# Context attentions of a two-layer perceiver: partial sums of the third head group joined on VectorE, weights of the last group summed in four parts

## The chip, the cores and the metric

The kernel runs on one core of a Trainium2 chip. A core has TensorE (PE in the profile; PEld is its weight load), VectorE (DVE), ScalarE (ACT), GpSimd (POOL), SyncE (SP, which here only issues DMAs) and 16 DMA engines. Matmuls write PSUM; all other data is in SBUF or in the chip's memory. The metric is the device time of one execution in microseconds (us), as the median of several runs.

## The reference

A batch of one, 512 query rows of 512 channels (`x`), a context of 8192 rows of 512 channels, and two layers. Each layer adds three things to `x`: a cross attention from `x` to the context, a self attention, and a mixture of 8 expert MLPs. The change touches only the two cross attentions, which have 16 heads of 32 channels each. The first is, cut to what matters (the second has no norm of q and k, and its mask comes from another input):

```python
q = _ln(q, qn_w, qn_b) * scale
k = _ln(k, kn_w, kn_b)
attn = jnp.einsum('bihd,bjhd->bhij', q, k)
attn = jnp.where(padding_mask[:, None, None, :], attn, -jnp.inf)
p = jax.nn.softmax(attn, axis=-1)
ctx = jnp.einsum('bhij,bjhd->bihd', p, v).reshape(b, s1, c)
out = ctx @ Wo.T + bo
```

The softmax needs, for each head and query, the sum of the exponentials over all keys (the denominator) and the sum of the exponentials times the values. The kernel forms both without dividing first, and divides at the end.

## The kernel before

Both attentions go through one function, `attend_slots`. It picks the tiles of 128 keys of the context that hold anything, at most 15 of them (`n = SLOTS = 15`), and works on the 16 heads in four groups of four (`NG = 4`, `GH = 4`). Its main loop runs over `at = 0 .. 59`, with `g, i = divmod(at, n)`: group `g`, key tile `i`. In the text (g, i) names a step of this loop; (3, 2) is the third key tile of the last group. One step does this:

- `score` (L939): four matmuls, one for each head, put 128 keys x 512 queries into four PSUM tiles `sc`. `subtract` (L800) takes off the largest score of each query. The four heads use different rows of the PE array and run side by side; a line "sc L939 x8" in the profile is four weight loads and four matmuls.
- `exp` (L1089): ScalarE turns each `sc` into a quarter of the SBUF tile `pT` (128 x 2048 numbers). `pT` has 5 buffers.
- For the group after, TensorE also makes scores the other way round (`scm`, L957), of which VectorE takes the maxima. These run ahead of their group, so the end of group 2 and all of group 3 have none.
- `accumulate` (L1044): four matmuls, side by side in different columns of the array, multiply `pT` with the values. For groups 0 to 2 each step has its own PSUM tile, which VectorE adds to the SBUF tile `o` (L1052). Group 3 sums in one PSUM tile `k.sums`. Where no `scm` are left, a step does this for the `pT` of two steps before (`accumulate(2)`).
- `add_up` (L1063): adds the `pT` of up to four steps into one tile `four` (5 buffers), on GpSimd for groups 0 to 2 and on VectorE for group 3. What is left is the list `parts[g]`. For groups 0 to 2 it has five members: steps 0-3, 4-7, 8-11, 12-13, and 14 alone. For group 3 it has six: 0-3, 4-7, 8-11, and 12, 13 and 14 alone.
- `denominators` (L1072): for each member of `parts[g]` four matmuls with a matrix of ones, side by side in the columns of the array, sum over the keys into one PSUM tile `den`.

Work of a group that is finished is put into `fillers` with the step at which it is due; each step takes at most one. For groups 0 to 2 these are `denominators` (L1127, due 3 steps after the group's last step; ScalarE then takes the logarithm of `den`, L1078), `divide` (4 steps after: an exponential on ScalarE, L1083, then a product and an added bias on GpSimd, L1084 and L1086), and `outputs` (L889, the product with the output weights, which VectorE adds to `x`, L895; for group 2 due 13 and 14 steps after). So group 2's denominators come in step (3, 2) and its outputs in steps (3, 12) and (3, 13).

The last group's denominators are written out by hand: two parts after step (3, 13), two after (3, 14), then `accumulate` for step 13, the last two parts, and `accumulate` for step 14. Then `finish_part` (L859 calls `divided`, L848) does two halves of 256 queries one after the other: logarithm and exponential of the denominator on ScalarE (`inverse`, L202 and L203), the product on VectorE (L850), the bias on ScalarE (L853). The four `outputs` of the last group and the norm of `x` follow.

A planner orders the instructions. Each engine gets a list; from the order of the program, the planner takes the first instruction that is ready by its own estimate of times, so one that would have to wait is passed by others. Each engine then works through its list. `tc.issue_after(ins)` puts everything traced inside it behind `ins` on the same engine; `pin` keeps the program's order.

PSUM tiles come from two sets, 4 of tag "s" and 3 of tag "m". `tile_s` takes them in a cycle of seven, so a step's four `sc` tiles can be written about one step ahead of the exponentials.

## Time and profile before

| what | us |
|---|---|
| runs shown: median (lowest, highest) of 3 | 1437.43 (1436.31, 1438.10) |
| the profiled execution: its time | 1435.61 |
| the profiled execution: span, first to last instruction | 1433.70 |
| PE `den` L1072, 216 matmuls in both attentions, mean of one | 0.592 |
| DVE `four` L1063 (128x2048 added), x18, each | 2.29 |
| POOL `four` L1063 (128x2048 added), x60, each | 4.55 |
| POOL L1084 and L1086 in `divide`, each | 1.29 and 1.57 |
| DVE L1052 (128x512 added), each | 0.68 |

The span is what the trace shows; the time has 1.91 us more that lie around it. The first attention's last group runs from about 344 to 394 us of the span, the second's from about 1103 to 1153 us.

How to read it: the chain of waits is the work that ended last, followed back from the end; a line has its start, its length, the engine, the tile and the line of the program. The timeline has every instruction, with the idle time of its engine before it and what ended it in square brackets. In both, neighbours of one kind are merged, and "x" counts them.

### The profile page before, as it was taken

What the parts mean: (1) busy time and instruction counts of PE and PEld (TensorE: products, weight loads), DVE (VectorE), ACT (ScalarE), POOL (GpSimd) and SP (SyncE); (2) the same over time, 40 slices, a digit from 0 to 9 for tenths busy, and PEclk for the clock granted to TensorE, in tenths of its full rate; (3) what the DMA queues carried; (4) which work ended last, traced back from release to release, by engine and by line L of the source; (5) the groups of instructions that cost most, each with busy time, mean ns of one, the idle gap of its engine ahead of it and who ended that gap; (6) DMA issues with size and microseconds to landing.
All of it is one profiled execution on the core that took longest, in us unless ns stands there. A gap on an engine that the chain in (4) does not pass through costs nothing.

```text
span 1433.7 us, 24957 instructions
## 1 busy us (share of the span) xinstructions
PE 1401.6 (98%) x9797; PEld 860.4 (60%) x9797; DVE 695.5 (49%) x1983; ACT 583.1 (41%) x1168; POOL 425.2 (30%) x359
## 2 busy tenths in 40 slices
PE   7989999999999999999999999999999999999997
PEld 3434444443244558999999766644444235499993
DVE  5558598985523424111111226769886525741112
ACT  2657466667732353111111131157667732321221
POOL 2150078987010110200001110058988010020002
PEclk9999999999999999999999999999999999989999
DMA  8455200000050005987889451000000050068575
GB/s 249 153 190 150 74 31 1 1 2 1 2 212 1 16 16 186 389 307 263 273 280 298 160 174 30 30 1 1 2 1 2 1 191 1 2 237 328 197 248 184
DMA packets 94267, 175.15 MB, mean 122 GB/s; under 512 B 5496, under 2 KB 32182, under 8 KB 92348
## 3 DMA queue, kind: packets, MB, share of 16 engines
q1 hardware_dynamic: 87004, 151.43, 31.5%
q0 software_dynamic: 6416, 19.94, 3.9%
q10 hardware_dynamic: 720, 2.10, 0.4%
q8 instruction: 79, 1.29, 0.4%
q14 instruction: 48, 0.39, 0.1%
HBM read 162.72 MB, written 9.68 MB: 120 GB/s over the span
## 4 chain that ended last, share of the span: by engine, by line
PE 88%; DVE 2%; ACT 1%; DMA 1%; issue 1%; POOL 0%; POOLq 0%; ACTq 0%
PE hps L2364 12%; PE y L2385 12%; PE sc L939 11%; PE acc L1044 8%; PE prj L1612 4%; PE pk L1421 4%; PE ops L889 4%; PE scm L957 4%; PE sc L957 3%; PE pv L1233 3%; PE den L1072 3%; PE pva L1548 2%; PE sc L800 2%; PE pk L1233 1%; PE y L2342 1%; PE pv L1457 1%
## 5 line engine op out<-in xcount | busy, mean ns | idle before, releaser
L1089 ACT ACTIVATE pT<-sc,kbias 128x512 f32<-128x512 f32 x480 | 288.3, 708 | 96.2 <-PE sc L800 85.7
L968 DVE CUSTOM_DVE_ANT_0 masked<-scm,krowb 128x512 f32<-128x512 f32 (+2 forms) x400 | 213.9, 591 | 40.0 <-PE scm L957 38.1
L939 PE MATMUL sc<-qTf,kTf 32*128 32x512 f32 x960 | 216.8, 621 | 1.5 <-DVE tops L968 1.5
L2364 PE MATMUL hps<-tokens,w 128*128 128x160 f32 (+11 forms) x1408 | 193.3, 293 | 0.0
L957 PE MATMUL scm<-kTf,qTf 32*128 32x512 f32 (+2 forms) x800 | 189.3, 539 | 0.0
L2364 PEld LDWEIGHTS hps<-tokens,w 128*128 128x128 f32 x1408 | 184.1, 191 | 2.7 <-issue 1.0
L2385 PE MATMUL y<-hT,w 128*128 128x160 f32 (+11 forms) x1280 | 176.2, 296 | 0.0
L2385 PEld LDWEIGHTS y<-hT,w 128*128 128x128 f32 x1280 | 169.7, 192 | 2.5 <-issue 0.8
L1063 POOL TENSOR_TENSOR four<-four,pT 128x2048 f32<-128x2048 f32 x36 | 163.9, 4553 | 1.6
L939 PEld LDWEIGHTS sc<-qTf,kTf 32*128 32x128 f32 x960 | 73.6, 183 | 95.7 <-DVE tops L968 42.5
L1044 PE MATMUL acc<-pT,vNf 128*32 128x512 f32 x960 | 127.8, 604 | 0.0
L968 DVE CUSTOM_DVE_ANT_0 masked<-sc,krowb 128x512 f32<-128x512 f32 (+2 forms) x176 | 98.6, 614 | 55.8 <-PE sc L957 55.2
L1063 POOL TENSOR_TENSOR four<-pT 128x2048 f32<-128x2048 f32 x24 | 109.3, 4554 | 54.1 <-ACT pT L1089 54.1
L2623 DVE TENSOR_TENSOR hT<-sg,hps 128x264 f32<-128x264 f32 (+7 forms) x64 | 28.0, 437 | 191.7 <-ACT sg L2622 177.1
L2622 ACT ACTIVATE sg<-hps 128x264 f32<-128x264 f32 (+7 forms) x64 | 25.3, 396 | 174.5 <-PE hps L2364 169.7
L957 PEld LDWEIGHTS scm<-kTf,qTf 32*128 32x128 f32 x800 | 86.1, 184 | 15.5 <-issue 6.3
L800 PE MATMUL sc<-shift,ones 3*128 3x512 bf16 (+3 forms) x544 | 93.2, 367 | 0.0
L2416 POOL DMA_DIRECT2D answers_d<-yb x17 | 9.6, 564 | 240.8 <-ACT yb L2403 240.8
L1052 DVE TENSOR_TENSOR o<-o,acc 128x512 f32<-128x512 f32 x84 | 57.3, 682 | 20.4 <-PE acc L1044 20.4
L1044 PEld LDWEIGHTS acc<-pT,vNf 128*32 128x32 f32 x960 | 19.3, 108 | 70.3 <-DVE tops L968 34.7
L1233 PE MATMUL pv<-wkvf,cslot 128*128 128x512 f32 x120 | 55.6, 613 | 3.0 <-issue 1.9
L1421 PE MATMUL pk<-cslot,wkf 128*128 128x256 f32 (+1 forms) x256 | 55.5, 370 | 0.0
(390 smaller groups left out, 1828.8 us busy)
## 6 DMA issues: line engine op xcount, KB each, us to landing
w<-in_L_ffn_W SPq DMA_DIRECT2D x94, 1024.0 KB, 6.6
mi<-in_mask SPq DMA_DIRECT2D x32, 512.0 KB, 4.2
cslot<-in_ctxT SPq DMA_DIRECT2D x40, 256.0 KB, 3.3
answers_d<-yb POOLq DMA_DIRECT2D x13, 256.0 KB, 4.6
answers_d<-zero POOLq DMA_DIRECT2D x9, 256.0 KB, 3.0
wkvf<-in_L_xattn_WkvT SPq DMA_DIRECT2D x8, 256.0 KB, 6.6
wof<-in_L_xattn_WoT SPq DMA_DIRECT2D x2, 1024.0 KB
wide<-in_L_attn_wk SPq DMA_DIRECT2D x4, 512.0 KB, 5.6
```

The source lines that it names most:

```text
L800: nc.tensor.matmul(ps, lhsT=ones16[r, :], rhs=k.shifts[g][r, 0:w], start=start, stop=stop)
L889: nc.tensor.matmul(ps, lhsT=k.o[g][:, t * P : (t + 1) * P], rhs=wo()[:, g, :], start=not direct, stop=True)
L939: nc.tensor.matmul(ps, lhsT=kT[HD * h : HD * (h + 1), g, i * P : (i + 1) * P], rhs=qT[HD * h : HD * (h + 1), g, :], start=True, stop=stop,)
L957: nc.tensor.matmul(ps[:, at : at + w], lhsT=qT[HD * h : HD * (h + 1), g, t * P : (t + 1) * P], rhs=kT[HD * h : HD * (h + 1), g, lo : lo + ...
L968: nc.vector.tensor_tensor_reduce(masked[:, 0:w], ps[:, at : at + w], krow[:, lo : lo + w], 1.0, -BIG, ALU.add, ALU.max, accum_out=tops[g % ...
L1044: nc.tensor.matmul(acc[HD * h : HD * (h + 1), :], lhsT=vN[:, i, g * P + HD * h : g * P + HD * (h + 1)], rhs=pT[:, h, :], start=alone or i ...
L1063: engine.tensor_tensor(to, parts[g][-1], pT, ALU.add)
L1089: nc.scalar.activation(pT[:, h, :], ps, AF.Exp, bias=kbias[:, i : i + 1])
L1233: last = nc.tensor.matmul(ps.rearrange("p (g n) -> p g n", g=NG), lhsT=src[:, c, s % 2, :], rhs=wkv[:, :, c, i * P : (i + 1) * P], start=( ...
L1421: end = nc.tensor.matmul(ps[:, j], lhsT=wk[:, g, c], rhs=src[:, c], start=(c == 0), stop=(c == NC - 1))
L2364: end = nc.tensor.matmul(ps[:, j, 0:k], lhsT=w1[:, c, f * P : (f + 1) * P], rhs=tokens[:, c, starts[r] : starts[r] + k], start=(c == 0), s ...
L2385: nc.tensor.matmul(accs[0][:, d, 0:k], lhsT=w2[:, f, d * P : (d + 1) * P], rhs=hT[:, f, 0:k], start=(c == 0 and f == 0 and d % 2 == 0), st ...
```

## The change

It touches the second half of `attend_slots` and two small functions above it.

- Group 2, joining: in step (3, 1), behind the addition of the group's last values (`k.added`, the last L1052), VectorE adds part 14 to part 12-13 (`join(2, 3, 4)`), then does step (3, 1)'s own `add_up`, then adds part 0-3 to part 4-7 (`join(2, 1, 0)`). `issue_after` fixes this order on VectorE. `parts[2]` is left with three members instead of five: 0-7, 8-11, 12-14.
- Group 2, due times: its denominators are due 4 steps after the group's last step instead of 3, and `divide` 5 instead of 4. Groups 0 and 1 keep theirs.
- Group 2, dividing: the product and the bias in `divide` go to VectorE instead of GpSimd.
- Group 3, joining: after the additions of steps 7 and 11 VectorE joins two parts each time, so that `parts[3]` ends with four members, 0-11, 12, 13 and 14, instead of six.
- Group 3, the end: no denominators after steps (3, 13) and (3, 14). After the loop come `accumulate` for step 13, the denominators of 12, 13 and 14, `accumulate` for step 14, and the denominators of 0-11.
- Group 3, dividing: both halves' `inverse` come first, then both halves' product and bias.

```diff
         def add_up(g, i, pT):
 
-            engine = nc.gpsimd if g < NG - 1 else nc.vector
-            if i % 4 == 0 or i >= (n - 1 if g < NG - 1 else (n - 1) // 4 * 4):
+            final = g == NG - 1
+            if i % 4 == 0 or i >= n - (3 if final else 1):
                 parts[g].append(pT)
                 return
...
-            engine.tensor_tensor(to, parts[g][-1], pT, ALU.add)
+            added = (nc.vector if final else nc.gpsimd).tensor_tensor(to, parts[g][-1], pT, ALU.add)
             parts[g][-1] = to
+            if final and i in (n // 2, n - 4):
+                join(g, 1, 0)
+            return added
+
+        def join(g, to, of):
+
+            ins = nc.vector.tensor_tensor(parts[g][to], parts[g][to], parts[g][of], ALU.add)
+            parts[g].pop(of)
+            return ins
...
         def divide(g):
 
             nc.scalar.activation(dens[g], dens[g], AF.Exp, scale=-1.0)
+            if g == NG - 2:
+                nc.vector.tensor_tensor(k.o[g], k.o[g], dens[g], ALU.mult)
+                nc.vector.tensor_scalar(k.o[g], k.o[g], bv[:, g : g + 1], None, ALU.add)
+                return
...
-            add_up(g, i, pT)
+            if g == NG - 1 and i == 1:
+                with tc.issue_after(k.added.ins):
+                    joined = join(NG - 2, 3, 4)
+                    with tc.issue_after(joined.ins):
+                        late_add = add_up(g, i, pT)
+                        with tc.issue_after(late_add.ins):
+                            join(NG - 2, 1, 0)
+            else:
+                add_up(g, i, pT)
             if i == n - 1 and g < NG - 1:
+                rest = 4 if g == NG - 2 else 3
                 fillers.extend((
-                    (at + 3, lambda g=g: denominators(g, range(len(parts[g])), len(parts[g]))),
-                    (at + 4, lambda g=g: divide(g)),
+                    (at + rest, lambda g=g: denominators(g, range(len(parts[g])))),
+                    (at + rest + 1, lambda g=g: divide(g)),
...
-            if g == NG - 1 and i >= n - 2:
-
-                lone = n - (n - 1) // 4 * 4
-                whole = (n - 1) // 4
-                end = whole + lone
-                denominators(g, range(0, whole - 1) if i == n - 2 else range(whole - 1, end - 2), end)
         accumulate(1)
-        denominators(NG - 1, range(end - 2, end), end)
+        denominators(NG - 1, (1, 2, 3), True, False)
         accumulate(1)
+        denominators(NG - 1, (0,), False, True)
         for _, f in fillers:
             f()
+        r = slice(0, S // 2), slice(S // 2, S)
+        d = late().tile([P, S], F32, name="d", tag="d", bufs=1)
+        k.o[NG - 1] = late().tile([P, S], F32, name="o", tag="o", bufs=2)
         for i in range(2):
-            r = slice(i * S // 2, (i + 1) * S // 2)
-            k.finish_part(NG - 1, r, k.sums[NG - 1][:, r], dens[NG - 1][:, r])
+            inverse(d[:, r[i]], dens[NG - 1][:, r[i]])
+        for i in range(2):
+            k.divided(NG - 1, r[i], d[:, r[i]], k.sums[NG - 1][:, r[i]])
         k.outputs(NG - 1, range(NT))
```

More of the change, by code (lines that the diff above doesn't have):

```diff
@@ L846, in begin, with divided @@
             k.sums[g] = [pacc.tile([P, S], F32, name=name, tag=name) for name in ("acc", "den")]
-        def divided(g, r, d, acc, den):
-            inverse(d[:, r], den)
-            nc.vector.tensor_tensor(k.o[g][:, r], acc, d[:, r], ALU.mult)
+        def divided(g, r, d, acc):
+            nc.vector.tensor_tensor(k.o[g][:, r], acc, d, ALU.mult)
             if bv is not None:
@@ L858, in finish_part @@
                 k.o[g] = late().tile([P, S], F32, name="o", tag="o", bufs=2)
-            divided(g, r, late().tile([P, S], F32, name="d", tag="d", bufs=1), acc, den)
+            d = late().tile([P, S], F32, name="d", tag="d", bufs=1)
+            inverse(d[:, r], den)
+            divided(g, r, d[:, r], acc)
         def finish(g, pieces=1):
@@ L895, in outputs @@
                     nc.vector.tensor_tensor(x[:, t, :], x[:, t, :], ps, ALU.add)
-        k.tile_s, k.subtract, k.shift_of = tile_s, subtract, shift_of
+        k.tile_s, k.subtract, k.shift_of, k.divided = tile_s, subtract, shift_of, divided
         k.begin, k.finish, k.finish_part, k.outputs, k.quotient = begin, finish, finish_part, outputs, quotient
@@ L1051, in accumulate @@
             elif alone:
-                nc.vector.tensor_tensor(k.o[g], k.o[g], acc, ALU.add)
+                k.added = nc.vector.tensor_tensor(k.o[g], k.o[g], acc, ALU.add)
         def add_up(g, i, pT):
-            engine = nc.gpsimd if g < NG - 1 else nc.vector
-            if i % 4 == 0 or i >= (n - 1 if g < NG - 1 else (n - 1) // 4 * 4):
+            final = g == NG - 1
+            if i % 4 == 0 or i >= n - (3 if final else 1):
                 parts[g].append(pT)
@@ L1062, in add_up, with denominators @@
                 to = late().tile([P, GH, S], F32, name="four", tag="four", bufs=5)
-            engine.tensor_tensor(to, parts[g][-1], pT, ALU.add)
+            added = (nc.vector if final else nc.gpsimd).tensor_tensor(to, parts[g][-1], pT, ALU.add)
             parts[g][-1] = to
-        def denominators(g, which, end):
+            if final and i in (n // 2, n - 4):
[5 more added lines that the diff above has]
+            return ins
+        def denominators(g, which, first=True, last=True):
+            if first:
+                dens[g] = tile_s(name="den")
             for j in which:
-                if j == 0:
-                    dens[g] = tile_s(name="den")
                 for h in range(GH):
@@ L1073, in denominators @@
                         dens[g][HD * h : HD * (h + 1), :], lhsT=k.ones32, rhs=parts[g][j][:, h, :],
-                        start=(j == 0), stop=(j == end - 1),
+                        start=first and j == which[0], stop=last and j == which[-1],
                     )
@@ L1135, in attend_slots @@
                 fillers.pop(0)[1]()
-            if g == NG - 1 and i >= n - 2:
-                lone = n - (n - 1) // 4 * 4
-                whole = (n - 1) // 4
-                end = whole + lone
-                denominators(g, range(0, whole - 1) if i == n - 2 else range(whole - 1, end - 2), end)
         accumulate(1)
-        denominators(NG - 1, range(end - 2, end), end)
+        denominators(NG - 1, (1, 2, 3), True, False)
         accumulate(1)
+        denominators(NG - 1, (0,), False, True)
         for _, f in fillers:
             f()
+        r = slice(0, S // 2), slice(S // 2, S)
+        d = late().tile([P, S], F32, name="d", tag="d", bufs=1)
+        k.o[NG - 1] = late().tile([P, S], F32, name="o", tag="o", bufs=2)
         for i in range(2):
-            r = slice(i * S // 2, (i + 1) * S // 2)
-            k.finish_part(NG - 1, r, k.sums[NG - 1][:, r], dens[NG - 1][:, r])
+            inverse(d[:, r[i]], dens[NG - 1][:, r[i]])
+        for i in range(2):
+            k.divided(NG - 1, r[i], d[:, r[i]], k.sums[NG - 1][:, r[i]])
         k.outputs(NG - 1, range(NT))
```

## The prediction

> **What bounds the kernel now.** I read the page's busy times and chain first, then the chain of waits and the timeline in the last head group of both context attentions, and last the busy times of one stretch. The page:

> ```profile
> PE 1401.6 (98%) x9797; PEld 860.4 (60%) x9797; DVE 695.5 (49%) x1983; ACT 583.1 (41%) x1168; POOL 425.2 (30%) x359
> PE 88%; DVE 2%; ACT 1%; DMA 1%; issue 1%; POOL 0%; POOLq 0%; ACTq 0%
> ```

> TensorE is the bound almost everywhere, so matmuls taken away can count, if nothing else holds the stage. The chain of waits in the second attention's last group (start, us, work):

> ```profile
> 1109.84 4.29 PE den L1072 x40
> ...
> 1143.12 1.85 PE den L1072 x16
> 1144.97 1.07 PE sc L939 x8
> 1146.05 0.22 PE sc L800 x4
> 1146.26 0.99 PE acc L1044 x8
> 1147.26 1.72 PE den L1072 x16
> 1148.98 0.86 PE acc L1044 x8
> 1149.83 1.84 PE den L1072 x16
> ...
> 1151.76 0.39 ACT d L202
> ...
> 1153.08 0.52 ACT o L853
> ```

> Group 2's five parts take 4.29 us in one piece, 0.858 a part; the last group's six take 1.85 + 1.72 + 1.84 in three pieces. A plain step is 1.07 + 0.22 + 0.99 = 2.28 us. The first attention has the same lengths (4.29 at 351.39; 1.85, 1.72 and 1.84 at the end). The timeline says what the other engines do meanwhile:

> ```profile
> 1102.80 4.55 POOL L1063 TENSOR_TENSOR four<-pT 128x2048 f32<-128x2048 f32 x1
> 1107.63 0.69 DVE L1052 TENSOR_TENSOR o<-o,acc 128x512 f32<-128x512 f32 x1 [1.59 <-PE acc L1044]
> 1109.18 2.29 DVE L1063 TENSOR_TENSOR four<-pT 128x2048 f32<-128x2048 f32 x1 [0.87 <-ACT pT L1089]
> 1111.57 2.29 DVE L1063 TENSOR_TENSOR four<-four,pT 128x2048 f32<-128x2048 f32 x1
> 1114.20 0.60 ACT L1078 ACTIVATE d<-den 128x512 f32<-128x512 f32 x1 [2.80 <-PE den L1072]
> 1114.83 0.63 ACT L1083 ACTIVATE d<-d 128x512 f32<-128x512 f32 x1
> 1115.44 23.23 ACT L1089 ACTIVATE pT<-sc,kbias 128x512 f32<-128x512 f32 x40
> ```

> While TensorE does the 4.29 us, ScalarE runs dry for 2.80. After it, 40 exponentials run without a gap: (23.23 - 0.71) / 39 = 0.577 us apart, 2.31 a step, hardly slower than TensorE's 2.28. ScalarE is a second bound, close behind. The stretch from the last addition of group 2's values to the last addition of its outputs (us, then busy PE, PEld, DVE, ACT, POOL with counts, granted clock, DMA share, GB/s):

> ```profile
> 1107.63:1142.65 35.02, 35.02 (x288) 9.56 (x288) 22.86 (x13) 30.62 (x53) 2.84 (x2) 1.00 0.01 2
> ```

> VectorE has 12.2 us free there, and the change fills them.

> **Part by part.**

> *Group 2's denominators.* Two parts fewer: 2 x 0.858 = 1.72 us of TensorE per attention. It is worth that much only if ScalarE can use it. From (3, 2)'s exponentials at about 1109.1 (a run of 26 ends at 1111.41, its last four took 2.3) it has eleven steps to do up to (3, 12) and 1.24 us of logarithm and exponential: 11 x 2.31 + 1.24 = 26.7, so it could end at 1135.8 where it ended at 1138.67. That is 2.9 us of room, more than 1.72. Taken: 1.72; bounds 0 (ScalarE holds the pace) and 1.72.

> [...]

> *Group 2's joins.* They run on VectorE behind the L1052 that ends at 1108.32. Their inputs are there: GpSimd's last part ends at 1107.35, the exponentials of (2, 14) are older. One 128x2048 addition behind another takes 2.35 (a pair is shown at 1124.98 with 4.69). First join, the addition of (3, 1), second join: 1108.32 + 3 x 2.35 = 1115.4. Queued behind them are the additions of (3, 2) and (3, 3), which end at about 1117.7 and 1120.1 instead of 1113.9 and 1120.2; they free `pT` buffers that are written five steps later, after 1122, so nobody waits.

> But the denominators due in (3, 3) need the second join first, and TensorE comes to them at 1109.84 + 2.28 = 1112.1, before the join ends. The planner passes over what isn't ready: in the trace ScalarE's logarithm and exponential of `divide` stand ahead of exponentials that come before them in the program (1114.20 against 1115.44). So I expect the scores of (3, 4) and (3, 5) ahead of `den`, the 2.57 us of `den` at about 1115.7, and no idle TensorE. If the planner's times err, TensorE stands up to the difference; cost taken 0, bounds 0 to 3.3 an attention.

> *Divide on VectorE.* GpSimd's 1.28 + 1.57 go; the product is like L1052 (0.69), the bias between the 0.55 and 0.81 of the 128x512 L259: 1.2 to 1.5 on VectorE. Hidden: `o` is ready at about 1121, the outputs come after 1135. Uncovered, it would cost its own 1.5.

> *Last group's joins.* Two additions of 2.29. VectorE in the stretch: 22.86 + 4 x 2.29 + 1.3 = 33.3, while the stretch shrinks to 35.02 - 1.72 = 33.3. It is exactly full. In order: the additions of 5, 6, 7 and the join end at 1130.6, those of 9, 10, 11 and the join at about 1140.0, the four outputs' additions (0.65 each) at 1142.7. What is late next is the PSUM of those outputs, which the scores of (3, 14) need at 1141.4 to 1141.8: of seven tiles four hold outputs and three are free, so one output must be added before, and it is, at 1140.7. Cost 0 with 0.9 us to spare. The part 0-11 is needed last of all, at about 1148.

> *The end.* Before, from 1143.12 to ScalarE's start at 1151.76: six parts 1.85 + 1.72 + 1.84, a step 2.28, an accumulate 0.86, 0.09 of hand-over: 8.64. After: a step 2.28, accumulate 13 0.86, parts 12, 13, 14 2.57, accumulate 14 0.86, part 0-11 with its hand-over 0.98, 0.08: 7.63. Gain 1.01, less than two parts, because accumulate 14 used to run under ScalarE's logarithm and now stands ahead of it. Part 14 needs the last exponential, 1.29 + 2.42 = 3.7 us in; its turn comes at 4.9.

> *Both inverses first.* Before, the first half's bias starts 1.32 after ScalarE's first logarithm. Now the second logarithm and exponential come between: starts 0, 0.41, 0.73, 1.13 (a 0.51 instruction is followed 0.41 after its start, so neighbours overlap 0.1), bias at about 1.45. Loss 0.13, bounds 0.04 (full overlap) and 0.32 (none). The second half is ready no later, and VectorE's chain behind the first half sets the pace. The end gains 1.01 - 0.13 = 0.88; bounds 0.69 and 0.97.

> *DMAs.* None is added. SP's next weights waited for accumulate 14 (issued 394.06 and 1152.51). The last reader of the old tiles becomes part 0-11, which ends earlier than accumulate 14 did, so they move up with the chain or more.

> Sum: 2 x (1.72 + 0.88) = 5.2 us. The profiled execution took 1435.61 (span 1433.70, 1.91 around it): 1430.4. The runs' median is 1.82 above it, so 1437.43 - 5.2 = 1432.2.

> **Rivals.**

> *TensorE waits for the join (slower).* If the planner leaves `den` at its place, TensorE stands from 1112.1 to 1115.4, 3.3 us for 1.72 saved. With the end's 0.88 that is +0.7 an attention: 1438.8. From 2.6 us of standing on, an end of the join after 1114.7, the change loses; each microsecond more on VectorE costs 2. For it: the join ends later than that by the rows above; against it, the passing over just shown.

> [...]

> *ScalarE holds the pace.* The middle gains nothing, the end 0.88: 1437.43 - 1.8 = 1435.7. For it, 2.31 against 2.28; against it, the 2.80 idle.

> *VectorE is late.* If its list slips 2 us, the scores of (3, 14) wait 1.1: 2 x (2.60 - 1.1) = 3.0, 1434.4. For it, the sum of 33.3 in 33.3; against it, that few of its results are awaited.

> **How the numbers follow.** Forecast 0.56, at 1432.2, its own range 1430.5 to 1434. VectorE late 0.12, ScalarE 0.12, TensorE waiting 0.20, of which 0.12 beyond +0.2%, since its additions come behind a full VectorE. About 0.2% (2.9 us) is what a measurement can tell from no change. Faster: 0.56 and half of 0.12, 0.62; same: 0.06 + 0.12 + 0.08 = 0.26; slower 0.12. The range 1429.8 to 1437.8 takes in the first three cases with the runs' own spread of 1.8 and leaves most of the fourth out.

> **What would show it.** Right: `den` of group 2 as one piece of 2.57 us; ScalarE's idle time before L1078 near 1.1 instead of 2.80 (it has 4.29 - 2.80 = 1.49 in hand when `den` begins, and 2.57 - 1.49 = 1.1); `den` behind scores of (3, 4) or (3, 5); four parts at the end, ScalarE's first L202 at about 7.6 us after the last outputs. Wrong: an idle TensorE released by VectorE's `four` before L1072 or before the scores of (3, 14), or ScalarE without a gap from (3, 2) on.

## The result, and the profile after

| | before | after |
|---|---|---|
| median of the first runs, us | 1437.11 (4 runs, 1436.31 to 1438.10) | 1444.78 (4 runs, 1442.09 to 1446.60) |
| ratio | | 1.0044 [1.0029, 1.0060] |
| profiled execution: time, span, us | 1435.61, 1433.7 | 1444.87, 1443.1 |
| its mean granted clock | 0.993 | 0.988 |

The change makes the kernel slower by 7.7 us. Timed again on two chips it was slower by 7.7 and 5.6 us: 1.0051 [1.0032, 1.0071] and 1.0048 [1.0030, 1.0066]. Below, the third group is group 2 of the code and the last group is group 3.

The page of after, busy times and shares of the chain that ended last by engine:

```profile
PE 1403.6 (97%) x9733; PEld 861.4 (60%) x9733; DVE 718.6 (50%) x1995; ACT 582.7 (40%) x1168; POOL 419.0 (29%) x355
PE 84%; DVE 3%; DMA 2%; issue 2%; ACT 1%; POOL 1%; POOLq 0%; SPq 0%; DVEq 0%; ACTq 0%
```

TensorE executes 64 matmul records fewer and is busy 2.0 us longer, so what is left took more time a piece. Each of these matmuls stands in the trace as two records (ten that are put in below appear as x20). So "sc x8" in the chain is four matmuls in eight records, and not four weight loads and four matmuls, as the section on the kernel before has it. `den` has 336 records before, 168 matmuls in both attentions, and not 216. The counts below are records: the 40 and 24 of the third group's `den` are 20 and 12 matmuls. The chain of waits of after, second attention, from the third group's last values on (start, us, work):

```profile
1113.70 0.54 issue
1114.24 2.29 DVE four L1072
1116.53 2.20 DVE four L1064
1118.73 2.21 DVE four L1072
1120.94 0.04 issue
1120.98 4.32 PE den L1082 x24
1125.31 1.07 PE sc L940 x8
```

The chain leaves TensorE and runs over VectorE: join, late addition, join, then `den`. `den` now has 24 records instead of 40, and yet takes 4.32 us where 40 took 4.29. The timeline of after has the same matmuls in both attentions, the first with the scores and values ahead of them (start, us, instruction, count, idle time before and what ended it):

```profile
352.45 1.22 PE L940 MATMUL sc<-qTf,kTf 32*128 32x512 f32 x7
353.41 0.39 PE L800 MATMUL sc<-shift,ones 3*128 3x512 bf16 x3
353.51 0.59 PE L940 MATMUL sc<-qTf,kTf 32*128 32x512 f32 x1
353.94 0.38 PE L800 MATMUL sc<-shift,ones 3*128 3x512 bf16 x1
354.24 1.06 PE L1045 MATMUL acc<-pT,vNf 128*32 128x512 f32 x8
357.65 2.78 PE L1082 MATMUL den<-four,ones 128*32 128x512 f32 x24 [2.34 <-DVE four L1072]
...
1120.98 4.32 PE L1082 MATMUL den<-four,ones 128*32 128x512 f32 x24 [2.35 <-DVE four L1072]
```

Both times TensorE stands idle for 2.34 us until the join ends; such an idle stretch is called a stand from here on. In the first attention the 24 then take 2.78, in the second 4.32. There the granted clock is 0.50 from 1120.73 us on for 3.41 us, a half-clock stretch; in the first attention it stays 1.00. ScalarE in the second attention of after:

```profile
1125.38 0.60 ACT L1088 ACTIVATE d<-den 128x512 f32<-128x512 f32 x1 [5.43 <-PE den L1082]
1126.01 0.63 ACT L1093 ACTIVATE d<-d 128x512 f32<-128x512 f32 x1
1126.62 20.91 ACT L1103 ACTIVATE pT<-sc,kbias 128x512 f32<-128x512 f32 x36
```

It runs dry for 5.43 us, where it was 2.80 before. The chain of waits at the end of the first attention, after:

```profile
387.11 1.07 PE sc L940 x8
388.18 0.22 PE sc L800 x4
388.40 1.85 PE acc L1045 x16
390.25 2.58 PE den L1082 x24
392.82 0.86 PE acc L1045 x8
393.68 0.86 PE den L1082 x8
```

The last group's four parts stand in the order that was forecast, with no wait between them.

I laid TensorE's accumulations and outputs of after against those of before, one by one, in the first attention. Ahead of the third group's `den` after is 1.13 us late (a half-clock stretch at 212.79 us, in code that is the same), behind it 2.47, at the last group's outputs 1.44. The stretch around the third group's `den` is called the middle, the one from there to the outputs the end: the middle costs 1.34 and the end gains 1.03. The 1.34 is the stand of 2.34, plus 0.5 in which the scores of (3, 3) wait for a PSUM tile, minus the 4.29 - 2.78 = 1.51 saved. The wait of 0.5 shows in the lines above: the fourth head's scores start alone at 353.51, when an exponential of ScalarE ends (353.50), and this step takes 2.78 us (from 351.46 to 354.24, values to values) where a plain one takes 2.28. In the second attention the middle costs 2.88, half clock included. At full clock the change would cost 2 x (1.34 - 1.03) = 0.6 us; some 5 to 7 us more are to be found.

### The profile page after: what moved, and what is told of

Its sections match the earlier page's. It is cut to its first block, busy times and chain, and to the rows that moved or that the text cites. A ratio compares the mean times of both kernels' runs of the same rounds, so it can differ in the third digit from the quotient of the medians.

```text
span 1443.1 us, 24827 instructions
## 1 busy us (share of the span) xinstructions
PE 1403.6 (97%) x9733; PEld 861.4 (60%) x9733; DVE 718.6 (50%) x1995; ACT 582.7 (40%) x1168; POOL 419.0 (29%) x355
## 3 DMA queue, kind: packets, MB, share of 16 engines
q8 instruction: 78, 1.28, 0.4%
## 4 chain that ended last, share of the span: by engine, by line
PE 84%; DVE 3%; DMA 2%; issue 2%; ACT 1%; POOL 1%; POOLq 0%; SPq 0%; DVEq 0%; ACTq 0%
PE hps L2386 11%; PE y L2407 11%; PE sc L940 10%; PE acc L1045 8%; PE prj L1634 4%; PE pk L1443 4%; PE scm L958 4%; PE ops L890 4%; PE sc L958 3%; PE pva L1570 2%; PE pv L1255 2%; PE den L1082 2%; PE sc L800 2%; PE y L2364 1%; PE vps L1821 1%
## 5 line engine op out<-in xcount | busy, mean ns | idle before, releaser
L800 PE MATMUL sc<-shift,ones 3*128 3x512 bf16 (+3 forms) x544 | 94.3, 368 | 0.0
L1255 PE MATMUL pk<-wkvf,cslot 128*128 128x512 f32 x120 | 56.3, 613 | 0.0
```

Source lines behind the costliest of these rows:

```text
L800: nc.tensor.matmul(ps, lhsT=ones16[r, :], rhs=k.shifts[g][r, 0:w], start=start, stop=stop)
L1255: last = nc.tensor.matmul(ps.rearrange("p (g n) -> p g n", g=NG), lhsT=src[:, c, s % 2, :], rhs=wkv[:, :, c, i * P : (i + 1) * P], start=( ...
```

## The experiments

Every kernel was timed beside the kernel before on the same chip. Times are medians, ratios with their 95% intervals.

**The kernel before, unaltered.**

> The kernel before, unchanged, as a control: its granted clock beside its time in several runs. In its profile the clock is at half in 4 stretches (one of them after the last matmul), in the changed kernel's in 10, and one more half-clock window of 3.4 us costs up to 1.7 us. Theory 'the wait' (the loss is TensorE standing 2.34 us in each attention for the join, and what follows from it): time 1437 +- 1 and clock 0.993 each time. Theory 'the windows' (most of the loss is half-clock windows that fall differently from run to run, whatever the code): the clock varies between 0.988 and 0.993 and the time between 1436 and 1444 with it, some 1.4 us for 0.001.

Measured: 1436.57 us, 0.9996 [0.9987, 1.0006]. A measurement of this size can tell some 1.5 us from nothing.

**The change with the denominators two tiles later.**

```diff
-                rest = 4 if g == NG - 2 else 3
+                rest = 6 if g == NG - 2 else 3
```

> The changed kernel with group 2's denominators due 6 steps after the group's last step instead of 4, and divide 7, so that the second join is done before TensorE comes to them. 'The wait': no idle TensorE ahead of group 2's den, 2 x 2.34 us of standing and 2 x 0.6 of held-up scores go, and the half-clock den of the second attention with them: 1437 or less, faster than the kernel before if the end's 2 x 1.0 gain is real. 'The windows': still 1440 to 1445 with a clock of 0.988 to 0.990. 'ScalarE holds the pace': no idle TensorE, but the middle gains nothing, about 1435 to 1438.

Measured: 1437.56, 0.9995 [0.9986, 1.0005]. The stand is gone, and with it the loss. Timeline of this kernel, first attention:

```profile
356.05 1.22 PE L940 MATMUL sc<-qTf,kTf 32*128 32x512 f32 x7
...
357.10 0.59 PE L940 MATMUL sc<-qTf,kTf 32*128 32x512 f32 x1
...
362.41 1.07 PE L1045 MATMUL acc<-pT,vNf 128*32 128x512 f32 x8
363.29 2.76 PE L1082 MATMUL den<-four,ones 128*32 128x512 f32 x24
```

`den` has no idle time before it. The middle gains 1.21 in both attentions, not the whole 1.72: the wait of 0.5 in the scores of (3, 3) is still there.

**The end alone**: the last group's four parts, its joins and both inverses first; the third group as before.

```diff
-            if g == NG - 2:
-                nc.vector.tensor_tensor(k.o[g], k.o[g], dens[g], ALU.mult)
-                nc.vector.tensor_scalar(k.o[g], k.o[g], bv[:, g : g + 1], None, ALU.add)
-                return
...
-            if g == NG - 1 and i == 1:
...
-            else:
-                add_up(g, i, pT)
+            add_up(g, i, pT)
...
-                rest = 4 if g == NG - 2 else 3
+                rest = 3
```

> The kernel before with the last group's end alone (four parts, two joins, both inverses first); group 2 as before. Predicted for this part: -0.88 an attention, read from the two traces: -1.03. 'The wait': 1437.1 - 2.1 = 1435.0. 'The windows': anything from 1434 to 1441, by its clock. A third theory, 'the end' (the new end costs time in what follows, by a longer idle TensorE before the norm): slower than 1438.

Measured: 1436.62, 0.9995 [0.9984, 1.0005]. Its trace gains 0.92 us at each of the two ends, 1.8 together, which is hardly more than the times can tell.

**The middle alone**: the third group's joins and divide as in the change, the last group as before.

```diff
-            if final and i in (n // 2, n - 4):
-                join(g, 1, 0)
...
+            if g == NG - 1 and i >= n - 2:
+                denominators(NG - 1, (0, 1) if i == n - 2 else (2, 3), i == n - 2, False)
...
-        denominators(NG - 1, (1, 2, 3), True, False)
+        denominators(NG - 1, (4, 5), False, True)
         accumulate(1)
-        denominators(NG - 1, (0,), False, True)
...
```

> The changed kernel with the last group's end as before (six parts, no joins in group 3, halves one after the other); group 2's joins, its due times and its divide as changed. 'The wait': the middle's +1.34 in each attention, and a den at half clock after 2.3 us of standing in one or both: 1437.1 + 2.7 to 1437.1 + 6.1, 1440 to 1443. 'The windows': the same middle, but the rest of the difference goes with the clock. 'The end': 1439.8 or less.

Measured: 1441.34, 1.0029 [1.0019, 1.0039]. The middle alone brings a loss of 4.2 us and the end alone none. Its trace has half clock straight behind both stands: `den` takes 4.23 and 4.08 us there, near the 4.32 above, and the middle costs 2.79 and 2.64 instead of 1.34. But the two halves of the change add up to 4.2 - 0.5 = 3.7 us, by the medians, where both together cost 5.6 to 7.7; what the rest is these two runs don't show.

**The change once more**, beside the next three.

> The changed kernel again, unaltered, on the chip and in the rounds of the three that follow. 'The wait' (TensorE stands 2.34 us ahead of the third group's denominators in each attention, and the granted clock halves behind it): 1444.8 again, 1442 to 1447, 1.003 to 1.006 of the kernel before. 'The windows' (the half-clock stretches fall where they like, and the four first runs of the change had more of them than is usual): 1437 to 1441.

Measured: 1446.02, 1.0051 [1.0032, 1.0071].

**The stand filled**: ten matmuls of the identity, which nobody reads, ahead of the denominators.

```diff
                 dens[g] = tile_s(name="den")
+                if g == NG - 2:
+                    for _ in range(10):
+                        tc.keep_in_program_order(nc.tensor.matmul(dens[g][:, 0:P], lhsT=ident, rhs=ident, start=True, stop=True))
```

> The changed kernel with ten 128x128 products of the identity (10 x 0.21 = 2.1 us of work that nobody reads) put on TensorE ahead of the third group's denominators, into the tile that these then overwrite: the join still ends when it did, the denominators still wait 0.2 us for it, but TensorE is busy through most of the 2.34 us. If the halved clock behind the stand is caused by the standing, and is worth 1.2 to 1.6 us an attention: 2.4 to 3.2 us less than the changed kernel, some 1441.5 against 1444.5, and a granted clock of 1.00 at the denominators. If the loss is the stand alone and the half clock is chance: the same as the changed kernel, within 0.7. Where the ten fillers end later than the join: up to 0.3 us an attention more.

Measured: 1439.08, 1.0007 [0.9995, 1.0019], 6.9 us below the change on the same chip. The join ends no earlier; TensorE only works meanwhile. Timeline of this kernel, second attention:

```profile
1113.91 2.50 PE L1082 MATMUL den<-ident 128*128 128x128 f32 x20
1116.34 2.78 PE L1085 MATMUL den<-four,ones 128*32 128x512 f32 x24
```

The idle time is gone and the 24 matmuls take 2.78. Against before the middle costs 1.35 in each attention and the end gains 1.03, so that + 0.6 is due; +0.7 was measured. The wait itself cost little here; what the filling takes away is the idleness. The filling was expected to bring 2.4 to 3.2 and brought more than twice that here, so it was timed again further down.

**One join moved early**, to the third group's thirteenth tile.

```diff
-                    joined = join(NG - 2, 3, 4)
+                    joined = join(NG - 2, 2, 3)
...
-                        with tc.issue_after(late_add.ins):
-                            join(NG - 2, 1, 0)
...
+            if g == NG - 2 and i == 12:
+                join(NG - 2, 1, 0)
```

> The changed kernel with the join of the third group's first two parts moved from the last of VectorE's three late operations to the third group's thirteenth tile, where VectorE has 1.8 to 2.7 us idle between two additions to o; the join of the last two parts stays at the last group's second tile and ends at 353.1 in the first attention, and TensorE reaches the denominators at 355.3. 'The wait': no stand of TensorE any more, den as one piece of 2.57 us without idle time; the time goes to that of the kernel with the denominators two tiles later (1437.6) or below, by the sum of the prediction to 1432. 'VectorE': the join at the thirteenth tile holds the next addition to o by up to 0.6 us and TensorE with it, 1 us more. 'The windows': no change from the changed kernel.

Measured: 1462.10, 1.0165 [1.0149, 1.0181]. None of the theories had this. Timeline of this kernel, first attention:

```profile
321.54 9.12 POOL L1064 TENSOR_TENSOR four<-four,pT 128x2048 f32<-128x2048 f32 x2
...
330.70 2.29 DVE L1072 TENSOR_TENSOR four<-four 128x2048 f32<-128x2048 f32 x1 [6.82 <-POOL four L1064]
...
333.73 1.22 PE L940 MATMUL sc<-qTf,kTf 32*128 32x512 f32 x1 [6.62 <-DVE tops L969]
```

VectorE had idle time there, but the join's input had not come: GpSimd, at 4.55 us an addition, was still adding it up. VectorE waited 6.82 with the maxima (`tops`) queued behind the join, and TensorE waited 6.62 for these. Behind this wait the scores that stand alone take 1.05 to 1.22 us, where one takes 0.59 at full clock (at 353.51 above); the mean granted clock of its runs is 0.9824 against 0.9923 of the kernel before beside them. Idle time of an engine is no place for an operation whose input is late.

**Both joins first, the late addition behind them.**

```diff
                     joined = join(NG - 2, 3, 4)
                     with tc.issue_after(joined.ins):
-                        late_add = add_up(g, i, pT)
-                        with tc.issue_after(late_add.ins):
-                            join(NG - 2, 1, 0)
+                        second = join(NG - 2, 1, 0)
+                        with tc.issue_after(second.ins):
+                            add_up(g, i, pT)
```

> The changed kernel with two of VectorE's three late operations changed about: both joins first, the last group's own late addition behind them. The second join then ends some 2.3 us earlier, at 355.3 in the first attention, when TensorE reaches the denominators (355.3): a stand of 0 to 0.2 us in place of 2.34. 'The wait': the same as with the join moved early, 1432 to 1438. If the late addition, now 2.2 us later, holds the last group's next parts or the buffers of its weights: a stand of ScalarE or TensorE later in the group, up to 2.2 us an attention. 'The windows': no change from the changed kernel.

Measured: 1437.58, 0.9986 [0.9975, 0.9996], 8.4 us below the change on the same chip. Chain of waits of this kernel, first attention:

```profile
351.12 4.50 DVE four L1072 x2
355.62 0.04 issue
355.66 2.78 PE den L1082 x24
358.44 1.07 PE sc L940 x8
```

The second join ends when TensorE arrives, the stand shrinks to 0.14 us, and the late addition is missed by nobody. The middle gains 0.87 in each attention of its trace.

**A stand put into the kernel before**: two operations of VectorE that change no value, behind the third group's last addition, on a part that the denominators read.

```diff
...
-            add_up(g, i, pT)
+            if g == NG - 1 and i == 1:
+                p = parts[NG - 2][0]
+                with tc.issue_after(k.added.ins):
+                    same = nc.vector.tensor_tensor(p, p, p, ALU.max)
+                    with tc.issue_after(same.ins):
+                        same = nc.vector.tensor_tensor(p[:, 0, :], p[:, 0, :], p[:, 0, :], ALU.max)
+                        with tc.issue_after(same.ins):
+                            add_up(g, i, pT)
+            else:
+                add_up(g, i, pT)
...
```

> The kernel before, all its sums and its 40 products of the third group's denominators kept, and two operations on VectorE added behind the third group's last addition to o, which put the greater of a value and itself back in its place (the first part whole, 2.3 us, and a quarter of it, 0.6): the denominators, at their old place, wait for them some 2.0 to 2.4 us from 351.4 on in the first attention, and likewise in the second. 'The stand alone': 2 x 2.0 to 2.4 = 4.0 to 4.8 us more than before, granted clock as before. 'The stand and the half clock behind it in two of three': 2 x 0.9 more, 6 to 6.6 more than before. If a stand brings more half-clock stretches elsewhere too, as the kernel with the filled stand hints (6.9 us better than the change, where two stretches of 1.4 are 2.8): 9 to 11 more than before and a mean granted clock below 0.991.

Measured: 1439.88, 1.0012 [1.0001, 1.0023]. The stand came out shorter than meant. Timeline of this kernel:

```profile
353.07 3.64 PE L1073 MATMUL den<-four,ones 128*32 128x512 f32 x32 [1.45 <-DVE four L1130]
```

TensorE stands 1.45 us and is delayed 1.66 in each attention, 3.3 together; no half clock follows in this trace (the 32 take 3.64 in both attentions, 3.62 in the kernel before), and the mean granted clock of its runs is 0.9932 against 0.9926 of the kernel before beside them. A stand this short cost its own time at most (2.0 us in the medians). One of 2.34 us was not tried in the kernel before.

**The same, filled** with the ten matmuls.

> The kernel with the added stand, and ten products of the identity (2.1 us) on TensorE ahead of the denominators, as before in the changed kernel: the denominators end as late as in the kernel with the stand at full clock. 'The stand alone': as the kernel with the stand, within 0.7. 'The half clock behind it': 4.0 to 4.8 more than before, 1.8 less than the kernel with the stand. 'Elsewhere too': 4.0 to 4.8 more than before, 5 to 6 less than the kernel with the stand, granted clock as before (0.992 to 0.993).

Measured: 1441.44, 1.0028 [1.0017, 1.0038]. The ten take 2.43 us, longer than the stand, and delay TensorE by 2.57 instead of 1.66: 2 x 0.91 = 1.8 us more, 1.6 measured. So filling paid nothing here, where no half clock followed the stand.

**Both joins first and the denominators one tile later** (`rest = 5`).

> Both joins first, and the third group's denominators and divide one tile later. 'The wait': the remaining stand of 0.3 us an attention goes, 0.6 us less than with the joins first alone, some 1436.9; the scores of the tile behind, which a late tile of PSUM holds up by 0.57 us, stay held. If the denominators at their later place hold ScalarE or the buffers: 0.5 to 1 us more.

Measured: 1439.31, 1.0006 [0.9997, 1.0016]. In its trace `den` is one piece of 2.58 without idle time and the middle gains 1.2. The 0.6 us that were expected over the joins first alone don't show: the median is 2.6 us above that of the next run, on the same chip, with intervals that overlap.

**Both joins first, again.**

> The kernel with both joins first a second time, beside the kernel before on this chip. By the traces' terms at full clock it gains 2 x (0.88 + 0.9) = 3.6 us, by its first run 0.8 [0.6 to 3.6]: 1434.5 to 1437.5, 0.997 to 0.9996 of before. If the half-clock stretches at 507 and 589 us of its first trace belong to the kernel: again there, and a clock near 0.991; if they are chance, on average 0.992 to 0.993 and a gain of 2 to 3.6 us.

Measured: 1436.75, 0.9997 [0.9982, 1.0012]. The mean granted clock of its runs is 0.9911, near the 0.991 expected if the stretches of the first trace belong to the kernel. Taken together this version takes the change's loss away; a gain over the kernel before is 1 us or so and not certain. Its terms promise 2 x (0.87 + 1.02) = 3.8; its runs have a mean clock of 0.991 where before had 0.992 to 0.993 beside them, which can eat up to 2 us of that.

**The change, both stands filled, the first alone, the second alone**, on another chip. The single fillings put the ten matmuls in where `phase` is not None, which is the first attention, or where it is None, the second.

> The changed kernel unaltered, on the chip and in the rounds of the three that follow, as their measure. 1444 to 1447, 1.004 to 1.007 of before, a mean granted clock of 0.988 to 0.990.

> Both stands filled, a second time: 1438 to 1440, 1.0000 to 1.0015 of before, clock 0.992 to 0.993, if the gain of 6.9 us of the first time is the filling's; 1441.5 to 1443 if it was 2.7 (the half-clock stretch straight behind each stand) and the rest luck.

> The changed kernel with ten products of the identity in the first attention's stand alone; the second's stays. 'Each stand costs its own half clock and no more' (1.4 us in two cases of three): 0.9 less than the changed kernel, 1444 to 1445. 'A stand has half-clock stretches behind it elsewhere too' (at 510 and 592 us behind the first, at 1168 behind the second): half of the 6.9 us, 1441 to 1443, and no more than chance at 510 and 592 of its trace.

> The second attention's stand filled, the first's left. 'Its own half clock and no more': 0.9 less than the changed kernel, 1444 to 1445. 'Elsewhere too': about half of the 6.9 us, 1441 to 1443, with the stretch at 1168 of the changed kernel's two traces gone and those at 510 and 592 kept.

| stands filled | median, us | ratio to before | mean granted clock of the runs |
|---|---|---|---|
| none | 1442.81 | 1.0048 [1.0030, 1.0066] | 0.9892 |
| first | 1440.33 | 1.0022 [1.0013, 1.0031] | 0.9917 |
| second | 1442.72 | 1.0035 [1.0022, 1.0047] | 0.9909 |
| both | 1440.12 | 1.0018 [1.0007, 1.0029] | 0.9922 |
| kernel before | 1437.22 | | 0.9932 |

Filling both is worth 2.7 us by the medians here, 6.9 on the chip above; the change has only six runs in each, spread over 9 to 10 us. The direction is the same twice, the size is not settled. The first stand's filling is worth more than the second's; the second's can't be told from nothing.

**Where the rest went.** The changed kernel's runs have a mean granted clock of 0.9887 to 0.9892, the kernel before beside them 0.9923 to 0.9932, a difference of 0.0036 to 0.0040. If TensorE lost all of it, that would be 5.8 us of 1440 at most. The runs themselves say less: over all recorded runs, among runs of one kernel, 0.001 of clock goes with some 1.1 us, so the difference is worth about 4 to 4.5 us (an estimate from the recorded times and clocks). With the 0.6 at full clock that is 5 of the 7 us, and about 2 stay open. So more than half of the loss goes with the clock.

Standing is a part of this, and not all. Straight behind the stands, 4 of 10 unfilled ones have a half-clock stretch, which costs 1.4 us each (`den` takes 4.08 to 4.32 there and 2.78 behind the others), 2 x 0.4 x 1.4 = 1.1 us; of the six filled ones none has (2.78 each). But versions without a stand lose clock too: 0.9909 against 0.9930 beside it with the denominators two tiles later, 0.9907 against 0.9926 with the joins first and the denominators one tile later, 0.9914 and 0.9911 against 0.9923 and 0.9926 with the joins first alone. That is 0.0010 to 0.0021, up to half of the change's loss of clock. With both stands filled it is nothing on one chip (0.9924 against 0.9923) and 0.0010 on the other. The other stretches lie elsewhere (after has some at 212.79, 509.75, 591.67 and 1168.52 us, while before has none from 99.20 to 1259.74), and no trace shows why they are more. This stays open.

## Why the prediction was wrong

It said 1432.2 and faster; its rival "TensorE waits for the join" came true.

- *Group 2's joins*, the step that failed: "The planner passes over what isn't ready ... So I expect the scores of (3, 4) and (3, 5) ahead of `den` ... and no idle TensorE", cost 0. `den` stayed at its place in the program, and TensorE stood 2.34 us in each attention. The evidence for passing over was ScalarE's logarithm and exponential ahead of older exponentials, and that is another engine and another case; no row showed it for TensorE. The bounds of 0 to 3.3 held the stand. That the wait for the join brings the loss is shown twice: later denominators and both joins first each take the wait away and bring the kernel back to the time of before. Filling the wait with work took off 6.9 us on one chip and 2.7 on another.
- *The rival's price.* It gave +0.7 an attention at full clock, a stand of 3.3 less 1.72 and 0.88; the trace has 1.34 - 1.03 = +0.3. The mechanism was right and the direct price near, though by terms that were each off (a stand of 2.34, 1.51 saved, 0.5 of scores held). What its sum left out is the clock, where some 4 of the 7 us went: 1438.8 was forecast for it and 1444.8 measured. Half clock didn't follow each stand: it followed 4 of 10 stands of 2.34 us, and ahead of two of these TensorE had been busy for 1.32 us (after, second attention) and 1.69 us (the second set of runs, first attention) of 3.41 us.
- *Group 2's denominators*, 1.72 saved. `den` as one piece takes 2.58 with the join early enough, as forecast, but only 1.2 of the 1.72 arrive. 0.5 go to the scores of (3, 3), whose PSUM tile ScalarE releases late (the start at 353.51 shown above): before, `den` took 4.29 us just ahead of these scores, and ScalarE ran dry for 2.80. This is the rival "ScalarE holds the pace" for not quite a third of the gain.
- *Divide on VectorE* and *the last group's joins* at no cost: right. The product and the bias take 0.69 + 0.49 and nobody is seen to wait; no scores wait for an output.
- *The end*, 0.88: measured 0.92 to 1.03. *Both inverses first*: the first bias at about 1.45 us behind the first logarithm was forecast, and 1.45 it is (394.61 to 396.06).
- *DMAs* move up with the chain or more: right. SP's first weights are issued at 393.79 instead of 394.06, while TensorE is 1.44 us late there.
- ScalarE's 0.577 us an exponential held (20.91 for 36).

## What to carry to other kernels

Work that is taken from the bounding engine and given to another pays only if its result is there when the bounding engine comes to it; find that time for each consumer, and order the helper's queue by it (here swapping two of VectorE's operations takes the whole loss away). A stand of TensorE can cost more than its length: behind 4 of 10 stands of 2.34 us the granted clock was halved, behind the two of 1.45 us it was not. Where a stand can't be avoided, matmuls that nobody reads are worth trying, if they are no longer than the stand. Times of one kernel differ by several microseconds between executions (the kernel before took 1435.00 to 1442.69 us beside the experiments, at mean granted clocks of 0.989 to 0.996), so a gain of 3 us needs many runs.

## What the runs showed of the hardware

```profile
506.34:509.75 3.41, 2.70 (x20) 0.96 (x20) 0.00 (x0) 3.38 (x8) 0.64 (x1) 1.00 0.00 0
509.75:513.16 3.41, 3.41 (x24) 0.90 (x16) 0.00 (x0) 0.16 (x1) 0.63 (x1) 0.50 0.02 5
```

```profile
505.39:508.80 3.41, 2.70 (x22) 1.09 (x24) 0.00 (x0) 3.11 (x8) 0.78 (x2) 1.00 0.00 0
508.80:512.21 3.41, 3.41 (x37) 1.14 (x30) 0.00 (x0) 1.21 (x4) 0.98 (x2) 1.00 0.00 0
```

TensorE is busy 2.70 of 3.41 us in both first windows, and only one is followed by half clock. Of the four stands of after and of the changed kernel's second set of runs, two have a line 0.25 us (after, second attention: 1120.73, the stand ends at 1120.98) and 0.62 us (second set, first attention: 357.05 and 357.67) before the stand's end, and half clock begins at this line. In the other two the line lies 1.50 us (after, first attention: 356.15 and 357.65) and 1.88 us (second set, second attention: 1121.64 and 1123.52) before the end, and none follows. Busy time alone doesn't decide. The windows of the second set of runs, the first and second attention's stand:

```profile
353.64:357.05 3.41, 1.69 (x14) 0.16 (x8) 3.41 (x2) 2.88 (x5) 0.00 (x0) 1.00 0.00 0
357.05:360.46 3.41, 2.79 (x16) 0.78 (x20) 3.31 (x3) 0.00 (x0) 0.00 (x0) 0.50 0.00 0
1121.64:1125.05 3.41, 1.53 (x16) 0.55 (x20) 3.41 (x2) 0.85 (x2) 0.00 (x0) 1.00 0.02 5
1125.05:1128.46 3.41, 3.41 (x32) 0.71 (x24) 3.31 (x3) 2.06 (x4) 0.00 (x0) 1.00 0.00 0
```

A window with 1.53 us of work, `den` behind the stand, keeps the full clock, and one with 1.69, scores and values ahead of it, doesn't. That a change which moves the later work by 1 us changes how many stretches lie behind it is a guess from these four stands; it may be part of what stays open, and was not tried.
